# A macaron block on one core: fp16 halves for the second low-rank matrix, the first base block's split moved, the bias added in two halves

## The chip, the cores and the metric

The kernel runs on one core of one Trainium2 chip. A core has a matrix engine (PE, with its weight loads shown as PEld), a vector engine (DVE), a scalar engine (ACT), a general engine (POOL) and a queue engine (SP) that here issues most of the transfers. They run side by side and wait for each other through semaphores. The metric is the device time of one execution in microseconds; the time before is the median of three runs.

## The reference: what is computed

The input x is 2 x 1024 tokens of 1024 features, float32. Three residual steps follow one another, each on a layer norm of x without weights:

```python
x = x + 0.5 * ffn(layernorm(x))
x = x + attention(layernorm(x))
x = x + 0.5 * ffn(layernorm(x))
```

The feed-forward step is a dense product with a bias and a mixture of eight low-rank pairs, of which a gate picks two per token:

```python
gate_logits = einsum('bsd,ed->bse', x, gate_w)            # 8 experts
weights, selected = top_k(gate_logits, 2)                 # softmax over the two
result = einsum('bsd,od->bso', x, base_w) + base_b        # 1024 x 1024
low = einsum('bsd,erd->ebsr', x, lora_A)                  # rank 16 per expert
lora_out = einsum('ebsr,eor,bse->bso', low, lora_B, w_full)
result = result + 2.0 * lora_out
```

Attention is causal, with 32 query heads and 8 key and value heads of 32 features and rotary positions. Both feed-forward steps use the same weights.

## The kernel before

**Tiles and precision.** The 2048 tokens are 16 tiles of 128. Dense products run in fp16 on split operands: a matrix is scaled by a power of two and written as a high half `hi` and a low half `lo = value - hi`, and a product is three matmuls, high by high, high by low, low by high (L361 to L363). `split` (L195) makes the halves of a weight: the high half on ACT (L200) or, for every fourth slice, on POOL (L197), the low half on DVE (L202). `pow2` (L167) finds the scale: squares summed on ACT (L171), the sum over all partitions with a small matmul (L176), a maximum on DVE (L178), a square root on POOL (L179), and then a few one-column operations that give the scale `S` and its inverse `INV` (L187).

**The feed-forward weights.** The base matrix is held in SBUF as two blocks of 512 output columns, `wb[:, n]`; `prep_base(n)` scales and splits block n in eight slices. `prep_gate` does the same for the gate and the first low-rank matrix together (`ag`). `prep_lora` splits the second low-rank matrix, 128 x 1024, into `lbh` and `lbl`. These two are of the type fp32r, a 4-byte type that PE takes, and are scaled with the base blocks' own scales, so that their product can be summed in the same PSUM bank.

**One feed-forward step** is `ffn` (L393), 32 times in all (16 tiles, two steps). First comes the gate product into `psa` (L395, the `misc` tile), then the bias is added to the tile's x on POOL (L396), and the gate's choice is worked out in some fifteen small operations (L399 to L419) that end in `lw`, the weighted low-rank activations. Then for each half n the dense product of 24 matmuls into `pd`, the transposed `lw` split into `lh` and `ll` (L434 to L438, once), three matmuls with `lbh` and `lbl` into the same bank (L441 to L443), and the update of x on DVE (L444), which needs the bias added.

**The layer norm** (`layernorm`, L331) takes statistics on DVE (L334, L336), a reciprocal root on POOL (L340), writes the normed tile on ACT (L352) and splits it: the high half on POOL (L313; for tiles 0 and 1 on ACT, L311), the low half on DVE (L314). A transposing transfer (L317) then brings both halves to the layout that PE needs (`tt`). The first three of these transfers and the loads traced before L776 are kept in SP's queue in program order.

**The order of the work.** The program is written as generators that are stepped by hand: in the prologue the weights are loaded, scaled and split while tiles 0 to 2 run their first step; in the main part, for each tile of attention, pieces of the dense stages are put between the attention units. Within what the program's order and its extra edges leave open, a planner orders the instructions of each engine at build time by priority and by its own estimate of their times. `tc.issue_after(ins)` adds an edge: what is traced inside comes behind `ins` on its engine. The prologue uses such edges: `marks` remembers the last layer norm's instructions, and in `prep_base(0)` the slices from the second on come behind tile 1's `xn` and `hi` on ACT and behind its `nb` and `lo` on DVE. In the program text the order of the prologue is: gate and first base block loaded, tile 1 loaded, layer norm of tile 0, gate prepared, second base block and second low-rank matrix loaded, tile 2 loaded, layer norm of tile 1, bias loaded, `prep_base(0)`, the key and value weights' loads on ACT's queue, `prep_base(1)`, `prep_lora`, the loads of Wo and of Wq's first half, layer norm of tile 2.

Of the kernel before, what the change touches and what calls it, by code (L numbers as in the profile page):

```python
# [9 lines left out]
FP = mybir.dt.float32  # L10
FPR = mybir.dt.float32r
HP = mybir.dt.float16
I32 = mybir.dt.int32
AF = mybir.ActivationFunctionType
# [26 lines left out]
def kernel(  # L41
# [94 lines left out]
    lbh = wres.tile([P, D], FPR)  # L136
    lbl = wres.tile([P, D], FPR)
# [29 lines left out]
    def pow2(aps, junk, name):  # L167

        am = small.tile([P, 2], FP, name="am")
        for j, (ap, jk) in enumerate(zip(aps, junk)):  # L170
            nc.scalar.activation(jk, ap, AF.Square, accum_out=am[:, j : j + 1])  # L171
        sq = small.tile([P, 1], FP, name="sq")
        nc.vector.tensor_tensor(sq, am[:, 0:1], am[:, 1:2], ALU.add)
        nc.vector.tensor_scalar(sq, sq, 2.0**-120, 2.0**120, ALU.max, ALU.min)
        every = p_s2.tile([P, GRP, P], FP, name="s2")[:, 0, :]
        nc.tensor.matmul(every, lhsT=sq.to_broadcast([P, P]), rhs=ident, start=True, stop=True)  # L176
        ar = small.tile([P, 1], FP, name="ar")
        nc.vector.tensor_reduce(ar, every, AX.X, ALU.max)  # L178
        nc.gpsimd.tensor_tensor(ar, ar, half, ALU.pow)  # L179
        e = small.tile([P, 1], FP, name="e")  # L180
        nc.vector.tensor_scalar(e.bitcast(I32), ar.bitcast(I32), 0x7F800000, None, ALU.bitwise_and)
        tag = "_".join(map(str, name))
        s = const.tile([P, 1], FP, name="s_" + tag)
        nc.vector.reciprocal(s, e)
        nc.vector.tensor_scalar(s, s, 16384.0, None, ALU.mult)
        inv = const.tile([P, 1], FP, name="i_" + tag)
        nc.gpsimd.tensor_scalar(inv, e, 1.0 / 16384.0, 0.0, ALU.mult, ALU.add)  # L187
        S[name], INV[name] = s, inv

    marks = {}  # L190

    def mark(name):
        return tc.issue_after(marks[name].ins) if name else nullcontext()

    def split(hi, lo, src, s, k, after=(None, None)):  # L195
        if k % 4 == 3:
            nc.gpsimd.tensor_scalar(hi, src, s, 0.0, ALU.mult, ALU.add)  # L197
        else:
            with mark(after[0]):
                nc.scalar.activation(hi, src, AF.Copy, scale=s)  # L200
        with mark(after[1]):
            nc.vector.scalar_tensor_tensor(lo, src, s, hi, ALU.mult, ALU.subtract)  # L202

    def prep_base(n, sts):
        pow2(sts, [wb[:, n, 0, h * HK : (h + 1) * HK, :] for h in range(2)], ("b", n))
        for k in range(KB):
            after = (None, None)
            if n == 0 and k > 0:
                after = ("xn", "nb") if k == 1 else ("hi", "lo")
            split(wb[:, n, 0, k, :], wb[:, n, 1, k, :], sts[k // HK][:, k % HK, :], S["b", n], k, after)  # L210
        u = const.tile([P, 1], FP, name=f"uf{n}")
        nc.gpsimd.tensor_scalar(u, INV["b", n], 0.5 / XS, 0.0, ALU.mult, ALU.add)
        S["uf", n] = u

    def prep_gate(sts):
# [6 lines left out]
        inva2 = const.tile([P, 1], FP)  # L222
        nc.gpsimd.tensor_scalar(inva2, INV["a",], 2.0, 0.0, ALU.mult, ALU.add)
        S["cg"], S["inva2"] = cg, inva2

    def prep_lora(st):
        for n in range(2):
            c = bass.ts(n, 512)
            nc.scalar.activation(lbh[:, c], st[:, c], AF.Copy, scale=S["b", n])
            nc.vector.scalar_tensor_tensor(  # L230
                lbl[:, c], st[:, c], S["b", n], lbh[:, c].bitcast(FP), ALU.mult, ALU.subtract
            )
        nc.scalar.mul(bb, bb, 0.5)
# [63 lines left out]
    class Split:  # L297
# [7 lines left out]
        def add(self, src, act=False):  # L305
# [4 lines left out]
            if act:  # L310
                marks["hi"] = nc.scalar.copy(hi, src)  # L311
            else:
                nc.gpsimd.tensor_scalar(hi, src, 1.0, 0.0, ALU.mult, ALU.add)  # L313
            marks["lo"] = nc.vector.tensor_tensor(self.hl[:, (2 * i + 1) * w : (2 * i + 2) * w], src, hi, ALU.subtract)  # L314
# [16 lines left out]
    def layernorm(xt, act=False, n=1):  # L331
# [15 lines left out]
        marks["nb"] = nc.vector.scalar_tensor_tensor(nb, mv[:, 0:1], -1.0, rs, ALU.mult, ALU.mult)  # L347
        xn = fpool.tile([P, D], FP, name="xn")
        sp = Split(n)
        for i in range(n):  # L350
            c = bass.ts(i, D // n)
            marks["xn"] = nc.scalar.activation(xn[:, c], xt[:, c], AF.Identity, bias=nb, scale=rs)  # L352
# [40 lines left out]
    def ffn(xt, tt, done):  # L393
        psa = p_misc.tile([P, 512], FP, name="misc")
        yield from dense(psa[:, 0 : P + E], tt, lambda k: (ag[:, 0, k, :], ag[:, 1, k, :]))  # L395
        nc.gpsimd.tensor_tensor(xt, xt, bb, ALU.add)  # L396
# [29 lines left out]
        for n in range(2):  # L426
# [5 lines left out]
            if n == 0:  # L432
                pst = p_misc.tile([P, 512], FP, name="misc")
                nc.tensor.transpose(pst[:, 0:P], lw.rearrange("p e r -> p (e r)"), ident)  # L434
                lh = small.tile([P, P], FPR, name="lh", bufs=LB)
                ll = small.tile([P, P], FPR, name="ll", bufs=LB)
                nc.scalar.copy(lh, pst[:, 0:P])
                nc.vector.tensor_tensor(ll, pst[:, 0:P], lh.bitcast(FP), ALU.subtract)  # L438
# [312 lines left out]
    gst = [agst[:, h] for h in range(2)]  # L751
    b0 = [piece(h - 2, [wb_in[:, 0:512]], h, nc.sync) for h in range(2)]
# [3 lines left out]
    prep_gate(gst)  # L756
    b1 = [piece(3 + h, [wb_in[:, 512:1024]], h, nc.sync) for h in range(2)]
    lst = xp.tile([P, D], FP, name="xt")
    pin(nc.sync.dma_start(out=lst, in_=lb_in))
# [3 lines left out]
    prep_base(0, b0)  # L763
# [239 lines left out]
```

## Time and profile before

| what | value |
|---|---|
| median of 3 runs (lowest, highest) | 1538.43 us (1531.92, 1540.04) |
| the profiled execution's own time | 1540.01 us |
| its span | 1538.2 us |
| mean granted PE clock | 0.984 |
| PE, DVE, ACT, POOL busy | 1434.5, 1080.9, 691.1, 480.0 us |
| first dense product of the base block starts | 25.80 us |
| first attention score matmul starts | 152.74 us |
| PE idle before the third dense product (DVE L444 ends it) | 43.61 to 53.05 us |

The page gives each engine's busy time and, in slices of 1/40 of the span, its busy share in tenths. The chain of work that ended last follows the program back from its last instruction to what released each step. A group row has the line, engine and operation, output and inputs by the program's names, shapes and types, the count, the busy time and mean duration, and after the bar the idle time of the engine just before, with what ended it. A row of waits has who waited for whom, the total in us, the times and the longest. A timeline row has the start and the duration in us, and in brackets the idle time before. Matmuls overlap in their pipeline, so the distance between starts tells their cost, not the duration.

### The profile page before, as it was taken

How to read it: one execution, taken by the hardware profiler on the slowest of the kernel's cores; microseconds unless marked ns; L12 is line 12 of the kernel's file. 1: busy time of each engine (PE TensorE's matmuls, PEld its weight loads, DVE VectorE, ACT ScalarE, POOL GpSimd, SP SyncE). 2: the span in 40 equal slices, each digit the busy share in tenths (PEclk: the TensorE clock that was granted, in tenths of full speed). 3: DMA queues.
4: the chain of work that ended last, by engine and by line, in shares of the span. 5: the costliest groups of instructions: out<-in, count | busy, mean ns of one | idle time of the engine just before them, and what ended most of it. 6: DMA issues, size and time to landing. Idle time of an engine off the chain costs nothing.

```text
span 1538.2 us, 39420 instructions
## 1 busy us (share of the span) xinstructions
PE 1434.5 (93%) x16594; PEld 846.2 (55%) x16594; DVE 1080.9 (70%) x2382; ACT 691.1 (45%) x1276; POOL 480.0 (31%) x678
## 2 busy tenths in 40 slices
PE   3687889899999999999999998999999999999997
PEld 2333445455656566666654454555656656666543
DVE  5968666958768577777664866867768577776553
ACT  7453334444444454454550334444445445555420
POOL 2544332524324133232131433433333232221221
PEclk9998999999999999999999999999999999999999
DMA  9776797969383763855647769566493753553551
GB/s 301 250 207 185 172 242 190 235 166 242 84 254 96 209 173 79 238 106 146 184 116 244 178 189 257 157 196 203 111 256 75 220 145 97 194 132 96 112 180 42
DMA packets 297186, 267.57 MB, mean 174 GB/s; under 512 B 262576, under 2 KB 265648, under 8 KB 276528
## 3 DMA queue, kind: packets, MB, share of 16 engines
q1 hardware_dynamic: 293456, 252.47, 61.5%
q10 hardware_dynamic: 3552, 12.58, 2.1%
q8 instruction: 130, 2.13, 0.6%
q14 instruction: 48, 0.39, 0.1%
HBM read 181.63 MB, written 20.45 MB: 131 GB/s over the span
## 4 chain that ended last, share of the span: by engine, by line
PE 70%; DVE 11%; DMA 10%; issue 3%; POOL 2%; ACT 2%; SPq 1%; ACTq 0%; DVEq 0%; POOLq 0%
PE av L630 14%; PE pd L361 12%; PE pd L362 12%; PE pd L363 12%; PE s L568 8%; PE s L683 7%; DMA qt<-qst 5%; DMA ws<-wstr 2%; DVE mx L585 2%; DVE hl L314 2%; DMA tt<-hl 2%; DVE rc L639 1%; PE pd L441 1%; PE pd L442 1%; PE pd L443 1%
## 5 line engine op out<-in xcount | busy, mean ns | idle before, releaser
L689 ACT ACTIVATE p<-s,cs 128x512 f32<-128x512 f32 x576 | 380.0, 688 | 279.4 <-PE s L683 276.2
L585 DVE TENSOR_REDUCE mx<-s 128x4 f32<-128x512 f32 x480 | 316.4, 676 | 182.0 <-PE s L568 155.9
L630 PE MATMUL av<-p,va 128*32 128x128 f32 x4608 | 236.6, 277 | 2.3 <-POOL p L691 1.3
L361 PE MATMUL pd<-ws,tt 128*128 128x512 f16 x592 | 225.4, 381 | 13.8 <-DMA ws<-wstr 9.4
L630 PE MATMUL av<-p,ones 128*32 128x128 f32 x4608 | 232.1, 273 | 0.0
L362 PE MATMUL pd<-ws,tt 128*128 128x512 f16 x592 | 225.2, 380 | 0.0
L363 PE MATMUL pd<-ws,tt 128*128 128x512 f16 x592 | 224.6, 380 | 0.0
L361 PEld LDWEIGHTS <-tt 128*128 128x128 f16 x1360 | 134.2, 99 | 163.3 <-DMA tt<-hl 28.1
L568 PE MATMUL s<-kts,qt 96*128 96x128 f16 x2304 | 200.0, 220 | 15.3 <-DMA qt<-qst 10.3
L361 PE MATMUL pd<-wb,tt 128*128 128x512 f16 x512 | 196.1, 383 | 17.2 <-DVE xt L444 11.7
L362 PEld LDWEIGHTS <-tt 128*128 128x128 f16 x1360 | 134.2, 99 | 140.4 <-issue 25.0
L683 PE MATMUL s<-qt,kts 128*128 128x512 f16 x576 | 201.9, 382 | 9.3 <-DMA qt<-qst 7.8
L568 PEld LDWEIGHTS <-qt 96*128 96x128 f16 x2304 | 149.9, 98 | 101.8 <-issue 37.7
L363 PEld LDWEIGHTS <-tt 128*128 128x128 f16 x1360 | 134.1, 99 | 129.3 <-issue 7.0
L362 PE MATMUL pd<-wb,tt 128*128 128x512 f16 x512 | 195.9, 383 | 2.2 <-DVE wb L202 2.2
L363 PE MATMUL pd<-wb,tt 128*128 128x512 f16 x512 | 195.7, 382 | 0.0
L630 PEld LDWEIGHTS av<-p,va 128*32 128x32 f32 x4608 | 122.4, 109 | 66.0 <-issue 54.8
L646 POOL TENSOR_TENSOR tt<-o,tt 128x128 f16<-128x128 f32 x128 | 62.7, 490 | 305.1 <-ACT tt L645 305.1
L691 POOL TENSOR_SCALAR_AFFINE_SELECT p<-p 128x512 f32<-128x512 f32 x128 | 85.9, 672 | 198.2 <-ACT p L689 197.1
L639 DVE RECIPROCAL rc<-o 128x128 f32<-128x128 f32 x128 | 121.0, 945 | 37.2 <-ACT o L637 36.9
L630 PEld LDWEIGHTS av<-p,ones 128*32 128x32 f32 x4608 | 138.2, 110 | 0.1
L580 POOL TENSOR_SCALAR_AFFINE_SELECT sm<-sm 128x512 f32<-128x512 f32 x96 | 67.8, 706 | 216.1 <-ACT sm L579 213.5
(164 smaller groups left out, 1815.6 us busy)
## 6 DMA issues: line engine op xcount, KB each, us to landing
ws<-wstr SPq DMA_DIRECT2D x148, 1024.0 KB, 5.9
wstr<-ws ACTq DMA_DIRECT2D x9, 1024.0 KB, 6.5
xt<-in_x_dram SPq DMA_DIRECT2D x16, 512.0 KB, 3.7
out_dram<-xt SPq DMA_DIRECT2D x15, 512.0 KB, 3.1
qt<-qst SPq DMA_TRANSPOSE x256, 3.0
ws<-in_wb_dram SPq DMA_DIRECT2D x2, 1024.0 KB, 8.4
qst<-in_wb_dram SPq DMA_DIRECT2D x2, 1024.0 KB, 7.9
st<-in_wo_dram SPq DMA_DIRECT2D x2, 1024.0 KB, 11.3
```

The lines of the kernel that those rows point to most:

```text
L361: nc.tensor.matmul(ps, lhsT=th, rhs=wh, start=(k == 0), stop=False)
L362: nc.tensor.matmul(ps, lhsT=th, rhs=wl, start=False, stop=False)
L363: nc.tensor.matmul(ps, lhsT=tl, rhs=wh, start=False, stop=(last and k == KB - 1))
L568: nc.tensor.matmul(ps[:, h, :], lhsT=q[0 : 3 * DH, h, :], rhs=KT[b0 + j][0 : 3 * DH, g, :], start=(not pem or h == 0), stop=not pem,)
L580: nc.gpsimd.affine_select(out=sm, in_=sm, compare_op=ALU.is_ge, fill=-3.0e38, base=0, pattern=[[0, GRP], [-1, P]], channel_multiplier=1,)
L585: nc.vector.tensor_reduce(mx[:, j, :], ps, AX.X, ALU.max)
L630: prev = nc.tensor.matmul(av[rows, i, :], lhsT=w, rhs=p32[:, h, :], start=(us[0][0] == 0 and n == 0 and i == 0), stop=(us[-1][0] == L - 1 ...
L639: nc.vector.reciprocal(rc, o[:, 1, :])
L646: nc.gpsimd.tensor_tensor(c.low(g), o2, c.high(g), ALU.subtract)
L683: ins = nc.tensor.matmul(ps.rearrange("p h k -> p (h k)"), lhsT=KT[b0 + j][:, g, :], rhs=q.rearrange("p h k -> p (h k)"), start=True, stop ...
L689: nc.scalar.activation(p32, ps, AF.Exp, scale=cs)
L691: nc.gpsimd.affine_select(out=p32, in_=p32, compare_op=ALU.is_ge, fill=0.0, base=0, pattern=[[0, GRP], [1, P]], channel_multiplier=-1,)
```

## The change

Three things are altered.

- **The second low-rank matrix in fp16.** `lbh`, `lbl`, `lh` and `ll` become fp16. The matrix gets a scale of its own (`pow2` on the loaded tile, name `l`), and so `pow2` has a new argument `least`, a floor under the base block's own measure: for block 0 it is worked out from `INV["a"]` and `INV["l"]`, for block 1 from `INV["b", 0]`. `inva2`, the factor in the gate's last step, now holds the low-rank scale and block 0's scale too, and `prep_lora` uses two column scales, `S["l"]` for the first half and `INV["b", 0] * S["l"] * S["b", 1]` for the second.
- **The prologue's order.** The second low-rank matrix is loaded ahead of the first base block instead of behind the second; its `pow2` comes behind `prep_gate`; `prep_base(0)` is written ahead of tile 2's load and of tile 1's layer norm; `marks` and the edges made with it are gone.
- **The bias** is added to the tile in two instructions of 512 columns instead of one of 1024.

```diff
--- before.py
+++ after.py
@@ -1,5 +1,5 @@
 from collections import deque
-from contextlib import ExitStack, nullcontext
+from contextlib import ExitStack
 
 import concourse.bass as bass
 import concourse.tile as tile
@@ -8,7 +8,6 @@
 from concourse._compat import with_exitstack
 
 FP = mybir.dt.float32
-FPR = mybir.dt.float32r
 HP = mybir.dt.float16
 I32 = mybir.dt.int32
 AF = mybir.ActivationFunctionType
@@ -133,8 +132,8 @@
 
     wb = wres.tile([P, 2, 2, KB, 512], HP)
     ag = wres.tile([P, 2, KB, P + E], HP)
-    lbh = wres.tile([P, D], FPR)
-    lbl = wres.tile([P, D], FPR)
+    lbh = wres.tile([P, D], HP)
+    lbl = wres.tile([P, D], HP)
     wstr = dram.tile([5, 2, P, 2, KB // 2, 512], HP)
     HK = KB // 2
     S, INV = {}, {}
@@ -164,7 +163,7 @@
             c += n
         return st
 
-    def pow2(aps, junk, name):
+    def pow2(aps, junk, name, least=None):
 
         am = small.tile([P, 2], FP, name="am")
         for j, (ap, jk) in enumerate(zip(aps, junk)):
@@ -179,6 +178,8 @@
         nc.gpsimd.tensor_tensor(ar, ar, half, ALU.pow)
         e = small.tile([P, 1], FP, name="e")
         nc.vector.tensor_scalar(e.bitcast(I32), ar.bitcast(I32), 0x7F800000, None, ALU.bitwise_and)
+        if least is not None:
+            nc.vector.tensor_tensor(e, e, least, ALU.max)
         tag = "_".join(map(str, name))
         s = const.tile([P, 1], FP, name="s_" + tag)
         nc.vector.reciprocal(s, e)
@@ -187,27 +188,28 @@
         nc.gpsimd.tensor_scalar(inv, e, 1.0 / 16384.0, 0.0, ALU.mult, ALU.add)
         S[name], INV[name] = s, inv
 
-    marks = {}
-
-    def mark(name):
-        return tc.issue_after(marks[name].ins) if name else nullcontext()
-
-    def split(hi, lo, src, s, k, after=(None, None)):
+    def split(hi, lo, src, s, k):
         if k % 4 == 3:
             nc.gpsimd.tensor_scalar(hi, src, s, 0.0, ALU.mult, ALU.add)
         else:
-            with mark(after[0]):
-                nc.scalar.activation(hi, src, AF.Copy, scale=s)
-        with mark(after[1]):
-            nc.vector.scalar_tensor_tensor(lo, src, s, hi, ALU.mult, ALU.subtract)
+            nc.scalar.activation(hi, src, AF.Copy, scale=s)
+        nc.vector.scalar_tensor_tensor(lo, src, s, hi, ALU.mult, ALU.subtract)
 
     def prep_base(n, sts):
-        pow2(sts, [wb[:, n, 0, h * HK : (h + 1) * HK, :] for h in range(2)], ("b", n))
+
+        least = const.tile([P, 1], FP, name=f"lb{n}")
+        if n == 0:
+            nc.vector.scalar_tensor_tensor(least, INV["a",], 2.0**32, INV["l",], ALU.mult, ALU.mult)
+        else:
+            nc.vector.tensor_scalar(least, INV["b", 0], 16384.0, None, ALU.mult)
+        pow2(sts, [wb[:, n, 0, h * HK : (h + 1) * HK, :] for h in range(2)], ("b", n), least)
+        if n == 0:
+            inva2 = const.tile([P, 1], FP)
+            nc.vector.scalar_tensor_tensor(inva2, INV["a",], 2.0, INV["l",], ALU.mult, ALU.mult)
+            nc.vector.tensor_tensor(inva2, inva2, S["b", 0], ALU.mult)
+            S["inva2"] = inva2
         for k in range(KB):
-            after = (None, None)
-            if n == 0 and k > 0:
-                after = ("xn", "nb") if k == 1 else ("hi", "lo")
-            split(wb[:, n, 0, k, :], wb[:, n, 1, k, :], sts[k // HK][:, k % HK, :], S["b", n], k, after)
+            split(wb[:, n, 0, k, :], wb[:, n, 1, k, :], sts[k // HK][:, k % HK, :], S["b", n], k)
         u = const.tile([P, 1], FP, name=f"uf{n}")
         nc.gpsimd.tensor_scalar(u, INV["b", n], 0.5 / XS, 0.0, ALU.mult, ALU.add)
         S["uf", n] = u
@@ -219,17 +221,16 @@
             split(ag[:, 0, k], ag[:, 1, k], sts[h], S["a",], 0)
         cg = const.tile([P, 1], FP)
         nc.gpsimd.tensor_scalar(cg, INV["a",], 1.0 / XS, 0.0, ALU.mult, ALU.add)
-        inva2 = const.tile([P, 1], FP)
-        nc.gpsimd.tensor_scalar(inva2, INV["a",], 2.0, 0.0, ALU.mult, ALU.add)
-        S["cg"], S["inva2"] = cg, inva2
+        S["cg"] = cg
 
     def prep_lora(st):
+        c = const.tile([P, 2], FP, name="sl")
+        nc.vector.tensor_copy(c[:, 0:1], S["l",])
+        nc.vector.scalar_tensor_tensor(c[:, 1:2], INV["b", 0], S["l",], S["b", 1], ALU.mult, ALU.mult)
         for n in range(2):
-            c = bass.ts(n, 512)
-            nc.scalar.activation(lbh[:, c], st[:, c], AF.Copy, scale=S["b", n])
-            nc.vector.scalar_tensor_tensor(
-                lbl[:, c], st[:, c], S["b", n], lbh[:, c].bitcast(FP), ALU.mult, ALU.subtract
-            )
+            h, s = bass.ts(n, 512), c[:, n : n + 1]
+            nc.scalar.activation(lbh[:, h], st[:, h], AF.Copy, scale=s)
+            nc.vector.scalar_tensor_tensor(lbl[:, h], st[:, h], s, lbh[:, h], ALU.mult, ALU.subtract)
         nc.scalar.mul(bb, bb, 0.5)
 
     KV = [wk_in, wv_in]
@@ -308,10 +309,10 @@
             src = src[:, i * w : (i + 1) * w]
             hi = self.hl[:, 2 * i * w : (2 * i + 1) * w]
             if act:
-                marks["hi"] = nc.scalar.copy(hi, src)
+                nc.scalar.copy(hi, src)
             else:
                 nc.gpsimd.tensor_scalar(hi, src, 1.0, 0.0, ALU.mult, ALU.add)
-            marks["lo"] = nc.vector.tensor_tensor(self.hl[:, (2 * i + 1) * w : (2 * i + 2) * w], src, hi, ALU.subtract)
+            nc.vector.tensor_tensor(self.hl[:, (2 * i + 1) * w : (2 * i + 2) * w], src, hi, ALU.subtract)
             m = 2 * KB // self.n
             pin(
                 nc.sync.dma_start_transpose(
@@ -344,12 +345,12 @@
         rs = small.tile([P, 1], FP, name="rs")
         nc.vector.tensor_tensor(rs, n1, r, ALU.mult)
         nb = small.tile([P, 1], FP, name="nb")
-        marks["nb"] = nc.vector.scalar_tensor_tensor(nb, mv[:, 0:1], -1.0, rs, ALU.mult, ALU.mult)
+        nc.vector.scalar_tensor_tensor(nb, mv[:, 0:1], -1.0, rs, ALU.mult, ALU.mult)
         xn = fpool.tile([P, D], FP, name="xn")
         sp = Split(n)
         for i in range(n):
             c = bass.ts(i, D // n)
-            marks["xn"] = nc.scalar.activation(xn[:, c], xt[:, c], AF.Identity, bias=nb, scale=rs)
+            nc.scalar.activation(xn[:, c], xt[:, c], AF.Identity, bias=nb, scale=rs)
             sp.add(xn, act)
         return sp
 
@@ -393,7 +394,9 @@
     def ffn(xt, tt, done):
         psa = p_misc.tile([P, 512], FP, name="misc")
         yield from dense(psa[:, 0 : P + E], tt, lambda k: (ag[:, 0, k, :], ag[:, 1, k, :]))
-        nc.gpsimd.tensor_tensor(xt, xt, bb, ALU.add)
+        for n in range(2):
+            c = bass.ts(n, 512)
+            nc.gpsimd.tensor_tensor(xt[:, c], xt[:, c], bb[:, c], ALU.add)
 
         lg = small.tile([P, E], FP, name="lg")
         nc.scalar.activation(lg, psa[:, P : P + E], AF.Copy, scale=S["cg"])
@@ -432,10 +435,10 @@
             if n == 0:
                 pst = p_misc.tile([P, 512], FP, name="misc")
                 nc.tensor.transpose(pst[:, 0:P], lw.rearrange("p e r -> p (e r)"), ident)
-                lh = small.tile([P, P], FPR, name="lh", bufs=LB)
-                ll = small.tile([P, P], FPR, name="ll", bufs=LB)
+                lh = small.tile([P, P], HP, name="lh", bufs=LB)
+                ll = small.tile([P, P], HP, name="ll", bufs=LB)
                 nc.scalar.copy(lh, pst[:, 0:P])
-                nc.vector.tensor_tensor(ll, pst[:, 0:P], lh.bitcast(FP), ALU.subtract)
+                nc.vector.tensor_tensor(ll, pst[:, 0:P], lh, ALU.subtract)
                 yield
             c = bass.ts(n, 512)
             nc.tensor.matmul(ps, lhsT=lh, rhs=lbh[:, c], start=False, stop=False)
@@ -749,18 +752,19 @@
                 )
             )
     gst = [agst[:, h] for h in range(2)]
+    lst = xp.tile([P, D], FP, name="xt")
+    pin(nc.sync.dma_start(out=lst, in_=lb_in))
     b0 = [piece(h - 2, [wb_in[:, 0:512]], h, nc.sync) for h in range(2)]
     load_x(1)
     a1 = [stage_a1(t) for t in range(3)]
     next(a1[0])
     prep_gate(gst)
+    pow2([lst[:, bass.ts(h, 512)] for h in range(2)], [lbh[:, bass.ts(h, 512)] for h in range(2)], ("l",))
     b1 = [piece(3 + h, [wb_in[:, 512:1024]], h, nc.sync) for h in range(2)]
-    lst = xp.tile([P, D], FP, name="xt")
-    pin(nc.sync.dma_start(out=lst, in_=lb_in))
+    prep_base(0, b0)
     load_x(2)
     next(a1[1])
     pin(nc.sync.dma_start(out=bb, in_=bias_in.partition_broadcast(P)))
-    prep_base(0, b0)
     stage(2, 0, 0, nc.scalar)
     stage(2, 1, 1, nc.scalar)
     prep_base(1, b1)
```

## The prediction

> **What bounds the kernel now.** I read four views: the page's shares and its slices, the engine totals cut at 160 and 300 us, the waits of PE in those stretches, and the groups and timelines of the touched lines. The page first:
>
> ```profile
> PE 1434.5 (93%) x16594; PEld 846.2 (55%) x16594; DVE 1080.9 (70%) x2382; ACT 691.1 (45%) x1276; POOL 480.0 (31%) x678
> PE   3687889899999999999999998999999999999997
> DVE  5968666958768577777664866867768577776553
> ```
>
> Each digit is 38.5 us. PE is short of work only in the first four slices. The totals cut by stage say the same: PE is busy 106.4 of the first 160 us, 124.2 of the next 140, and 1203.9 of the last 1238.2. So the kernel is a prologue that waits (53.6 us of idle PE) and a long stretch in which PE leaves only 34.3 us. A nanosecond of PE work taken out after 160 us is worth about 0.96 of itself (1328.1 busy of 1378.2); a wait taken from another engine is worth at most what PE idles for it. What PE waits for, first to 160 us, then from 300 us (total, times, longest):
>
> ```profile
> PE misc L361 <- DMA tt<-hl: 16.8, 2, 9.4
> PE pd L361 <- DVE xt L444: 11.7, 3, 9.4
> PE pd L361 <- ACT wb L200: 4.9, 1, 4.9
> ...
> PE misc L361 <- DMA tt<-hl: 4.4, 3, 2.1
> PE s L568 <- DVE mx L585: 2.8, 6, 0.8
> ```
>
> **Part 1: fp16 for the second low-rank matrix.** 3 matmuls of 128x512 in 64 blocks change type. The last two blocks stand side by side at the end of the PE timeline (start, duration):
>
> ```profile
> 1531.82 0.38 PE L362 MATMUL pd<-wb,tt 128*128 128x512 f16 x1
> 1532.04 0.38 PE L363 MATMUL pd<-wb,tt 128*128 128x512 f16 x1
> 1532.07 0.58 PE L441 MATMUL pd<-lbh,lh 128*128 128x512 f32 x1
> 1532.49 0.39 PE L442 MATMUL pd<-lbl,lh 128*128 128x512 f32 x1
> 1532.72 0.39 PE L441 MATMUL pd<-lbh,lh 128*128 128x512 f32 x1
> 1532.95 0.39 PE L442 MATMUL pd<-lbl,lh 128*128 128x512 f32 x1
> 1533.18 0.63 PE L443 MATMUL pd<-lbh,ll 128*128 128x512 f32 x2
> ```
>
> Read the starts, not the durations: the 0.58 only begins early. fp16 matmuls start 0.216 us apart, these 0.23. Six at 0.216 behind 1532.04 would end at 1532.04 + 6 x 0.216 + 0.38 = 1533.72; they end at 1533.81, so 0.045 us per triple. Where another matmul follows (159.68 to 160.83 us: L363, three of these, two of fp16) the spacing is 1.147 against 5 x 0.216 = 1.080: 0.067. The weight load of these takes 190 ns in the median (L441), that of fp16 98 to 99 ns. Here a rule is to be weighed. The Trainium skill (TensorE: Matmul & The Clock Gate, LDWEIGHTS) prices a load by its columns alone, 128/1.2 = 107 ns whatever the type, which would hide all of it and make this part worth 0; its section on weight-path modes excepts fp32 from the fast load. The row has 190 against 99, so I go by the rows: 64 x (0.045 to 0.067) = 2.9 to 4.3 us of PE, middle 3.5, times 0.96: **-3.3 us** (ends 0 and -4.3). L229, L230, L437 and L438 write fp16 in place of a 4-byte type: L200 and L202 do this at the same size (0.71 and 0.75 us against 0.71 and 0.72), so nothing.
>
> **Part 2: the bias add in halves.** In most blocks L396 follows L313 on POOL, and holds up the low half L314 on DVE, which feeds the transpose that PE waits for:
>
> ```profile
> 1343.84 1.04 POOL L313 TENSOR_SCALAR hl<-xn 128x1024 f16<-128x1024 f32 x1 [1.45 <-ACT xn L352]
> 1344.85 2.36 POOL L396 TENSOR_TENSOR xt<-xt,bb 128x1024 f32<-128x1024 f32 x1
> ...
> 1344.92 3.38 DVE L314 TENSOR_TENSOR hl<-xn,hl 128x1024 f16<-128x1024 f32 x1 [0.65 <-POOL hl L313]
> ```
>
> L314 takes 1.21 us when free. 20 of its 48 take over 2.5 us, 40.5 us above 1.21 in all. Size of a half: L646 does 128 elements in 0.42 us at the least, L396 1024 in 2.35, so 2.15 ns an element and 512 in 1.25; two are 0.15 dearer, 32 x 0.15 = 4.8 us on a POOL busy 31%. Does DVE get in between the halves? The Trainium skill (GPSIMD Engine Reference, Instruction dispatch) says that a following Pool instruction starts on each of its cores as soon as the share of the one before is done, no barrier between. Taken alone that lets the second half follow at once, and L314 ends 0.15 later than now: 32 x 0.15 = up to 4.8 us lost on DVE. The trace shows the case, three adds back to back:
>
> ```profile
> 41.30 8.29 POOL L396 TENSOR_TENSOR xt<-xt,bb 128x1024 f32<-128x1024 f32 x3
> ...
> 40.70 3.94 DVE L202 SCALAR_TENSOR_TENSOR wb<-qst,s_b,wb 128x512 f16<-128x512 f32 x2 [0.59 <-POOL wb L197]
> 44.77 6.04 DVE L202 SCALAR_TENSOR_TENSOR wb<-qst,s_b,wb 128x512 f16<-128x512 f32 x3
> ```
>
> An add here is 2.76 us apart instead of 2.35, and one L202 passes at each boundary (ends at 44.64, 47.40 and 50.14). So DVE does get in, and the later add waits. L314 then ends about 1.1 us earlier, 20 x 1.1 = 22 us of DVE. PE idles for few of them: behind the held L314 at 850.6 (idle 1.34 us), 1344.9 (0.84), 1511.4 (2.10, with the 4.2 us transpose between), around 282 to 292 (0.72 and 1.99), and behind L644 at 925.5 (2.05). At most 1.1 from each, and half of it for the last two: 1.1 + 0.84 + 1.1 + 1.1 + 0.6 = 4.7. Where a second such operation follows (L510 then L314 at 114; L595 then L314 at 872) the second half catches it and nothing is won. I take **-4 us**. Ends: +1 (POOL's 4.8 us on the path at the place of its 2% in the chain, or the rule) and -10 (L314 is 2% of the chain, 31 us, a third of that).
>
> **Part 3: the prologue.** *Added*: a scale for the second low-rank matrix. Two squares on ACT (like L171's 0.65 + 0.19 each): 1.7 us. DVE: some 14 small operations at 0.15 to 0.29 (sum, clamp, reduce, mask, two for the scale, the floor, the maximum twice, two for inva2, two for the pair of scales): 2.3 us. POOL a power (0.55) less one product (0.19); PE two small matmuls (0.77 at 9.34). Cover: ACT is idle 2.3 us before 19.18 and 1.6 before 22.03, DVE idle most of the time to 22 us, PE from 10.1 to 17.5; without it 2 to 3 us. On the path stay the maximum (0.15) and the data: 512 KB go ahead of the base block in SP's queue, 0.5 us of issue and at the 300 to 350 GB/s of those microseconds 1.5 to 1.7 of transfer. ACT is behind the data anyway (second square of block 0 at 14.90, landed 13.6), so the scale comes at about 23.0 instead of 22.34.
>
> *Moved*: eight splits of block 0 (six L200 of 0.71, two L197, eight L202 of 0.75) go ahead of tile 1's norm in program order and lose their order edges. ACT starts its six at 25.03 now, after one square and L311 of tile 1; it could start at 23.0. For: -2 us to the first dense product, which L200 and L202 hold (PE idle 4.87 and 2.16). Against: tile 1's L311 falls behind 3.8 us of ACT and its L314 behind 5.5 us of DVE, so its transpose leaves SP up to 5.5 us after 26.41. Behind it in SP's queue stand the bias and two Wo loads (31.6 to 33.6); the Wq loads wait till 50.2 for their buffer anyhow. The transpose lands at 35.1, and PE starts tile 1's product at 35.68, so PE is late by those 5.5. What hides this is the next hole: PE idles from 43.61 to 53.05, for L444, which stands on DVE behind all eight L202 of block 1. Gone, that cover costs 5.5. The adds at 41.3 shift with the bias, and L444 has 8 us of room after the first. **+1 us**, ends -3 and +7.
>
> **Sum.** -3.3 - 4 + 1 = -6.3 us. The profiled execution took 1540.0 (span 1538.2, 1.8 around it), 1.6 above the median: 1533.7 for it, 1538.4 - 6.3 = **1532 us** in the median. The planner makes the order anew from its own estimates, and a new order of the prologue is the part that no row prices.
>
> **Rivals.**
> - *The DVE release spreads* (faster): all of the 10 us of chain in L314 comes back, block 0 starts 2 us earlier, PE saves 3.8: -15.8, 1523 us. For: DVE is 11% of the chain, mostly attention maxima behind such rows. Against: PE idles only 34.3 us after 300.
> - *Tile 1 late* (slower): its norm falls behind the splits of block 0, and its product and gate come 5.5 us later; tile 1 then also enters the waiting row of three transposes at 111 to 139 us later, so the hole that hides it moves along instead of shrinking. Two such slips, 5.5 at 35 us and as much again at the 9.4 us hole before 122, less gains of 3, are +8 to +12: 1548 us. It decides once the slip passes what the 9.44 us hole covers. For: 16.8 us of PE waits for these transposes before 160. Against: the hole is bound by DVE, not by tile 1.
> - *Nothing arrives*: the loads are hidden as the rule has it, the second half catches what follows: 1538 us.
>
> **How the numbers follow.** The sum as worked out 0.36, the spread 0.26, tile 1 late 0.28, nothing 0.10. 0.5% is 7.7 us, about what a measurement here can tell from no change: bounds 1530.7 and 1546.1. Faster: 0.24 of the spread and 0.12 of the sum, 0.36. Slower: 0.24 of tile 1 late. Same 0.40. Range 1520 to 1550: the spread's centre less 3, the late case's centre plus 2; about 2 in 10 lie outside. The likeliest case by itself: 1526 to 1538.
>
> **What would show it.** Lora matmuls 0.216 apart with 99 ns loads; two L396 halves of 1.25 us with L314 ending near 2.2 us after its start; first dense product at 23.5 to 25.5 us; tile 1's transpose issued at 27 to 32; the hole before 53 us still ended by L444. Wrong if L314 stays at 3.4, or if first attention scores (152.7 now) come later than 157 or earlier than 148.

## The result and the profile after

The changed kernel takes 1525.88 us in the median of six runs (1522.40 to 1528.67), the kernel before 1538.62 in its six (1531.92 to 1540.09). The ratio is **0.9909**, 95% interval 0.9892 to 0.9926: about 14 us faster. The sum of the prediction was -6.3 and its time 1532. The profiled execution of after took 1522.65 us, span 1520.9, granted clock 0.985 against 0.984; it lies 17.4 below that of before, more than the ratio says, and parts read from single profiles below carry some us of scatter.

The shares of the page of after:

```profile
PE 1428.8 (94%) x16596; PEld 832.9 (55%) x16596; DVE 1067.4 (70%) x2396; ACT 691.1 (45%) x1280; POOL 496.6 (33%) x711
```

PE is busy 5.7 us less, and its idle time fell from 103.7 to 92.1. DVE does 14 instructions more and is busy 13.5 less; POOL is busy 16.6 more. Time that DVE stood under the adds thus went over to POOL. By the same stages as in the prediction, PE idles 49.4 us to 160 us (53.6 before), 14.8 from there to 300 (15.8), and 27.9 after that (34.3).

What PE waits for, first to 160 us, then from 300 us (total, times, longest):

```profile
PE s L175 <- DVE sq L173: 24.0, 5, 8.1
...
PE pd L362 <- DMA tt<-hl: 3.7, 1, 3.7
PE pd L362 <- DVE xt L447: 3.4, 1, 3.4
PE misc L362 <- DMA tt<-hl: 1.5, 1, 1.5
...
PE s L571 <- DVE mx L588: 2.1, 4, 0.8
...
PE misc L362 <- DMA tt<-hl: 1.5, 2, 1.1
```

The gate product's wait for a transpose (`misc`) went from 16.8 to 1.5 before 160 us and from 4.4 to 1.5 after 300; the 11.7 us behind the residual update are 3.4. But 24.0 us of waits for the sums of squares of weights (L173, in `pow2`) have come up in their place, so that PE idles in all only 4.2 less before 160 us; what is won there is that it is further on by then.

The end of the PE timeline of after (start, duration) and its loads for the low-rank matmuls (count, min/median/max ns):

```profile
1514.89 0.38 PE L364 MATMUL pd<-wb,tt 128*128 128x512 f16 x1
1515.11 0.38 PE L444 MATMUL pd<-lbh,lh 128*128 128x512 f16 x1
1515.33 0.38 PE L445 MATMUL pd<-lbl,lh 128*128 128x512 f16 x1
...
1515.97 0.59 PE L446 MATMUL pd<-lbh,ll 128*128 128x512 f16 x2
```

```profile
L444 PEld LDWEIGHTS <-lh x64: 95/98/99, 43.8 to 1515.3; 128*128 128x128 f16 x64
```

The spacing is the 0.216 us of the base product and the load is 98 ns, as forecast. A feed-forward step's layer norm near the end, POOL and DVE of after:

```profile
1495.53 1.04 POOL L314 TENSOR_SCALAR hl<-xn 128x1024 f16<-128x1024 f32 x1 [2.25 <-ACT xn L353]
1496.54 3.47 POOL L399 TENSOR_TENSOR xt<-xt,bb 128x512 f32<-128x512 f32 x2
1496.97 1.92 DVE L315 TENSOR_TENSOR hl<-xn,hl 128x1024 f16<-128x1024 f32 x1
```

The low half (L315) took 1.92 us here where the place shown of before took 3.38, and the two halves of the add took 3.47 together where the whole took 2.36: the second one waited for DVE. The same line over the whole run, before and after (min/median/max ns):

```profile
L314 DVE TENSOR_TENSOR hl<-xn,hl x48: 1159/1643/3387, 11.8 to 1511.4; 128x1024 f16<-128x1024 f32 x48
```

```profile
L315 DVE TENSOR_TENSOR hl<-xn,hl x48: 1160/1667/2299, 14.3 to 1497.0; 128x1024 f16<-128x1024 f32 x48
```

The median hasn't moved, but none is over 2.3 us, where 20 were over 2.5. Before, the 48 held 43.9 us above 1.21; after, 24.4.

### The profile page after: what moved, and what is told of

Its sections match the earlier page's. It is cut to its first block, busy times and chain, and to the rows that moved or that the text cites. A ratio compares the mean times of both kernels' runs of the same rounds, so it can differ in the third digit from the quotient of the medians.

```text
span 1520.9 us, 39480 instructions
## 1 busy us (share of the span) xinstructions
PE 1428.8 (94%) x16596; PEld 832.9 (55%) x16596; DVE 1067.4 (70%) x2396; ACT 691.1 (45%) x1280; POOL 496.6 (33%) x711
## 4 chain that ended last, share of the span: by engine, by line
PE 74%; DVE 10%; DMA 8%; issue 2%; POOL 2%; ACT 1%; SPq 1%; DVEq 0%; POOLq 0%; ACTq 0%
PE av L633 15%; PE pd L362 13%; PE pd L363 13%; PE pd L364 13%; PE s L571 8%; PE s L686 7%; DMA ws<-wstr 3%; DMA qt<-qst 3%; DVE ws L196 1%; DVE mx L588 1%; DVE hl L315 1%; DMA tt<-hl 1%; PE pd L444 1%; PE pd L446 1%; PE pd L445 1%
## 5 line engine op out<-in xcount | busy, mean ns | idle before, releaser
L649 POOL TENSOR_TENSOR tt<-o,tt 128x128 f16<-128x128 f32 x128 | 55.5, 434 | 295.6 <-ACT tt L648 295.5
L583 POOL TENSOR_SCALAR_AFFINE_SELECT sm<-sm 128x512 f32<-128x512 f32 x96 | 62.1, 647 | 204.2 <-ACT sm L582 203.9
```

Of the source, the lines that this page charges most:

```text
L583: nc.gpsimd.affine_select(out=sm, in_=sm, compare_op=ALU.is_ge, fill=-3.0e38, base=0, pattern=[[0, GRP], [-1, P]], channel_multiplier=1,)
L649: nc.gpsimd.tensor_tensor(c.low(g), o2, c.high(g), ALU.subtract)
```

## Experiments

Two theories stood against each other. **Release**: an add on POOL holds up the DVE instruction beside it, chiefly the low half, until the current POOL instruction ends; halves shorten the hold, and the time follows. **Order**: every edit makes the planner lay out the whole program anew, and a new order is worth some us by chance or by the moved prologue, whatever the halves do. Of the change's three edits, **h** is the add in halves, **t** the fp16 types, **o** all the rest: the low-rank matrix's own scale and earlier load, the moved split, no marks. All eight combinations were measured.

### The halves alone

```diff
-        nc.gpsimd.tensor_tensor(xt, xt, bb, ALU.add)
+        for c in (bass.ts(0, 512), bass.ts(1, 512)):
+            nc.gpsimd.tensor_tensor(xt[:, c], xt[:, c], bb[:, c], ALU.add)
```

> The kernel before with the bias add in two halves and nothing else. Theory 1 (prologue): the change won about 6 us before the main part, by the new order, and the halves only free PE where it idles behind a held low half: 4 us less than before, 1534.5. Theory 2 (release): the halves let DVE run earlier everywhere, prologue included, and are most of the change: 8 to 10 us less, 1529. L314 ends about 2.25 us after its start in both.

Measured: 1531.52 us against 1540.99, ratio 0.9932 (0.9915 to 0.9948). This one line brings about three quarters of the whole change. Its low halves:

```profile
L314 DVE TENSOR_TENSOR hl<-xn,hl x48: 1159/1646/2299, 11.2 to 1508.5; 128x1024 f16<-128x1024 f32 x48
```

### The types alone

```diff
-    lbh = wres.tile([P, D], FPR)
-    lbl = wres.tile([P, D], FPR)
+    lbh = wres.tile([P, D], HP)
+    lbl = wres.tile([P, D], HP)
...
-                lh = small.tile([P, P], FPR, name="lh", bufs=LB)
-                ll = small.tile([P, P], FPR, name="ll", bufs=LB)
+                lh = small.tile([P, P], HP, name="lh", bufs=LB)
+                ll = small.tile([P, P], HP, name="ll", bufs=LB)
```

> The kernel before with lbh, lbl, lh and ll in fp16 and nothing else (scales and order as before). Both theories: PE saves 2.9 to 4.3 us in the 192 matmuls, 3.3 us of it at the end, 1535. If the loads are hidden anyway: 1538.5.

Measured: 1539.95 against 1540.99, 0.9990 (0.9980 to 1.0000): 1 to 1.5 us, if anything, where 3.3 was forecast.

### The prologue alone

The changed kernel with the types of before and the whole add:

```diff
-        for n in range(2):
-            c = bass.ts(n, 512)
-            nc.gpsimd.tensor_tensor(xt[:, c], xt[:, c], bb[:, c], ALU.add)
+        nc.gpsimd.tensor_tensor(xt, xt, bb, ALU.add)
...
-    lbh = wres.tile([P, D], HP)
+    lbh = wres.tile([P, D], FPR)
```

> The changed kernel with the bias add whole and the 4-byte type put back, so that only the prologue's order, its loads and the scale of its own are changed against before. Theory 1: the first base block's splits end by 28 us and the second's by 44, PE's hole before 53 us shrinks, and 5 to 7 us less than before, 1532. Theory 2: tile 1's late transpose eats what the splits gain, within 2 us of before.

Measured: 1541.39 against 1540.99, 1.0005 (0.9992 to 1.0017). The first attention score starts at 145.9 us instead of 152.7, so the prologue is nearly 7 us ahead, and the end knows nothing of it. By tile 0's last score the lead is gone: it starts at 200.2, in before at 193.8. Between these two scores PE idles 11.4 us, in before 5.0. The waits of PE from 160 to 215 us, of o and then of before, and of SP's queue in o from 145 to 205:

```profile
PE pd L362 <- DMA ws<-wstr: 5.1, 2, 3.0
```

```profile
PE pd L361 <- DMA ws<-wstr: 1.2, 1, 1.2
```

```profile
SPq L374 <- DMA wstr<-ws: 11.3, 1, 11.3
```

PE waits there for weights (`ws`) read back from DRAM, and their load waits in SP's queue for the split weights to be written there. PE came earlier, the weights did not. The clock takes its part too: between the two scores its mean is 0.94 in o and 1.00 in before. That is two stretches of 3.4 us at half clock, which cost up to 3.4 us of work.

### The marks alone

The kernel before without its edges in `prep_base(0)`, as a control for the order:

```diff
-            if n == 0 and k > 0:
-                after = ("xn", "nb") if k == 1 else ("hi", "lo")
```

> The kernel before without its order edges (marks) on the first base block; the program's order, types and bias add as before. Theory 1 (the order of the first block decides): the split starts as soon as the scale is there, some 2 us earlier, and a part of the order's gain is seen, 2 to 4 us less than before. Theory 2 (edges don't matter, the planner had put tile 1's norm ahead in any case): within 2 us.

Measured: 1541.28, 1.0001 (0.9989 to 1.0012). A new order, the same time, and the same granted clock (0.984 in the mean).

### Two of three

The halves with the types: the edits of the first two experiments together, in before.

```diff
-    lbh = wres.tile([P, D], FPR)
+    lbh = wres.tile([P, D], HP)
...
-        nc.gpsimd.tensor_tensor(xt, xt, bb, ALU.add)
+        for c in (bass.ts(0, 512), bass.ts(1, 512)):
+            nc.gpsimd.tensor_tensor(xt[:, c], xt[:, c], bb[:, c], ALU.add)
```

> The kernel before with the halves and with fp16, the prologue's order, its scales and its loads as before. If the parts add up (halves alone 0.9932 of before, types alone 0.999): 0.992, 1529 against 1541. If the types pay in full only once PE no longer waits for the low halves: 0.990, that is the whole of the change.

Measured: 1529.44 against 1540.55, 0.9923 (0.9907 to 0.9938).

The halves with the prologue: the changed kernel with the four tiles of the low-rank product (`lbh`, `lbl`, `lh`, `ll`) of the 4-byte type.

```diff
-    lbh = wres.tile([P, D], HP)
+    lbh = wres.tile([P, D], FPR)
```

> The changed kernel with the 4-byte type put back: halves and the prologue's order. If the parts add up (halves 0.9932, order alone 1.0005): 0.9937, 1531. If the order pays only together with the halves, because without them the whole adds hold the splits of the second block: 0.991 or less.

Measured: 1529.02, 0.9919 (0.9906 to 0.9932).

The types with the prologue: the changed kernel with the whole add.

```diff
-        for n in range(2):
-            c = bass.ts(n, 512)
-            nc.gpsimd.tensor_tensor(xt[:, c], xt[:, c], bb[:, c], ALU.add)
+        nc.gpsimd.tensor_tensor(xt, xt, bb, ALU.add)
```

> The changed kernel with the bias add whole: fp16 and the prologue's order. If the parts add up: 0.9995, 1540. If order and types win something of their own that the halves don't need: 0.997 or less.

Measured: 1541.19, 1.0005 (0.9990 to 1.0021): **without the halves the change is worth nothing**.

The table cuts each profile into three. *Tail* goes from the start of the last score matmul (L683 in before) to the end of the last matmul; *body* from tile 2's last score matmul to the one where the tail begins; *head* is the rest of the span. The last column is the granted PE clock, as a share of the full clock, over all executions of a kernel; before has 0.9840 (19) on the chip of the kernels with two of three.

| kernel | ratio to before | head us | body us | tail us | granted clock, mean (runs) |
|---|---|---|---|---|---|
| before | 1 | 317.2 | 1169.5 | 51.5 | 0.9835 (51) |
| without marks | 1.0001 | 317.0 | 1168.1 | 51.6 | 0.9837 (13) |
| t | 0.9990 | 321.2 | 1168.6 | 51.3 | 0.9834 (21) |
| o | 1.0005 | 319.4 | 1172.1 | 51.4 | 0.9807 (21) |
| t and o | 1.0005 | 317.5 | 1168.5 | 49.7 | 0.9791 (14) |
| h | 0.9932 | 318.7 | 1166.2 | 47.6 | 0.9840 (6) |
| h and t | 0.9923 | 314.9 | 1163.0 | 47.4 | 0.9830 (6) |
| h and o | 0.9919 | 312.1 | 1165.0 | 47.4 | 0.9832 (5) |
| after (h, t and o) | 0.9909 | 311.9 | 1161.5 | 47.5 | 0.9845 (6) |

The five kernels with the whole add lie within 0.15% of each other, 2.3 us, each in an order of its own; the four with halves lie together 0.7 to 0.9% lower. So a new order by itself does not bring the change's time. It isn't without effect, though: o and t and o run at a lower granted clock than before on the same chip, by 0.0028 and 0.0049 (standard errors 0.0006 and 0.0009). Times 1541 us, this is up to 4.3 and 7.6 us that these orders win elsewhere and pay back in clock; the estimate is an upper one, since half clock costs nothing while PE idles. The kernels with halves run within 0.001 of the clock of before, so their gain is no gain of clock. Halves are worth 0.68% alone, 0.67% beside t, 0.86% beside o, 0.96% beside both (differences of the ratios; 0.1% is 1.5 us); the larger values beside o go with the clock that o loses without them. In the mean of four against that of five they gain 4.1 us in the head, 5.4 in the body and 3.6 in the tail. In the same means PE idles 5.6, 3.1 and 2.1 us less in these three, and loses up to 1.4, 1.0 and 1.4 us less to half clock; what PE does in head and body differs from kernel to kernel, so these parts don't add up to the gains. The tail is the firm one: its values agree to 0.3 us but for one kernel.

### Quarters

```diff
-        for n in range(2):
-            c = bass.ts(n, 512)
+        for n in range(4):
+            c = bass.ts(n, 256)
             nc.gpsimd.tensor_tensor(xt[:, c], xt[:, c], bb[:, c], ALU.add)
```

> The changed kernel with the bias add in four instructions of 256 columns. If the hold on the low half is what the halves took away, a quarter of 0.70 us lets L315 start 0.55 us earlier once more, so it ends near 1.7 us in place of 2.25, and half of the gain comes again: 2 to 4 us less than the changed kernel, at 0.988 of before. If the new order that the planner makes is what paid, the quarters land anywhere within 5 us of the changed kernel.

Measured: 1523.82 against 1540.55, 0.9883 (0.9863 to 0.9902), where after has 0.9909. The low half is nearly free, with 11.1 us above 1.21 left of 24.4:

```profile
L315 DVE TENSOR_TENSOR hl<-xn,hl x48: 1156/1241/1758, 14.1 to 1500.5; 128x1024 f16<-128x1024 f32 x48
```

### The whole add behind the low half

This takes the hold on the low half away with no halving: the add of before waits until the tile's low half is done.

```diff
-            marks["lo"] = nc.vector.tensor_tensor(...)
+            self.lo = marks["lo"] = nc.vector.tensor_tensor(...)
...
-        nc.gpsimd.tensor_tensor(xt, xt, bb, ALU.add)
+        add = nc.gpsimd.tensor_tensor(xt, xt, bb, ALU.add)
+        tc.add_manual_dep(add.ins, tt.lo.ins.name, ..., reason="low")
```

> The kernel before, its bias add whole, but made to wait for the low half of the tile's layer norm (L314). If the hold on the low half is what costs: no L314 is over 1.3 us any more, and at least the gain of the halves is there, 0.9932 of before or less, near 0.990. If the halves paid by the other order that the planner made of 32 more instructions, or by shorter holds on other DVE operations: the add now holds those for its full 2.35 us, and the time is within 3 us of before.

Measured: 1532.32 against 1541.15, 0.9941 (0.9920 to 0.9963), about the halves' gain with one instruction per add. Its low halves, and one add that waits:

```profile
L314 DVE TENSOR_TENSOR hl<-xn,hl x48: 1161/1225/1648, 11.2 to 1510.5; 128x1024 f16<-128x1024 f32 x48
```

```profile
1510.54 1.22 DVE L314 TENSOR_TENSOR hl<-xn,hl 128x1024 f16<-128x1024 f32 x1
...
1511.84 2.35 POOL L396 TENSOR_TENSOR xt<-xt,bb 128x1024 f32<-128x1024 f32 x1 [1.74 <-DVE hl L314]
```

So taking the hold off the low half is worth about 9 us in the order that this kernel got. Its low halves are not wholly free, as was expected: 12 of 48 take over 1.3 us (28 in before). But of the 43.9 us above 1.21 only 4.2 are left, where the halves leave 24.4 and win no less. Time does not follow the low half alone, then; the halves also shorten the holds on other DVE operations, and how much of their gain lies there is not shown. This kernel's granted clock is a little higher than that of before (0.9855 in the mean against 0.9834), by the same estimate up to 3.2 us of its gain. Its tail is 46.4 us, a little shorter than with halves.

### No bias add

The kernel before without the add. The bias is missing from the output, so this is not a faster kernel but the price of the add.

```diff
-        nc.gpsimd.tensor_tensor(xt, xt, bb, ALU.add)
```

> The kernel before without the bias add (L396 left out, so the bias is missing from the output; all else as before). It bounds what the add costs. If the low halves are all of it: as with the add behind the low half, 0.990 to 0.989. If DVE's other held operations count as much: 0.986 or less (of 69 us that DVE loses under the adds, 40 are the low halves').

Measured: 1521.07 against 1541.15, 0.9875 (0.9855 to 0.9895). The 32 adds cost about 19 us end to end, though POOL is busy 31% of the span. This lies between the two values expected, so the low halves are not all of it. Halves give back a good half of that, and the tail without any add (46.4 us) is that of the add behind the low half.

### The changed kernel with the add behind, whole and in quarters

```diff
-        for n in range(2):
-            c = bass.ts(n, 512)
-            nc.gpsimd.tensor_tensor(xt[:, c], xt[:, c], bb[:, c], ALU.add)
+        add = nc.gpsimd.tensor_tensor(xt, xt, bb, ALU.add)
+        tc.add_manual_dep(add.ins, tt.lo.ins.name, ..., reason="low")
```

> The changed kernel with the add whole again and made to wait for the low half (L315). If the hold on the low half decides: as fast as the changed kernel with its halves or 1 to 3 us faster, 0.989 to 0.991 of before. If it decides only because the halves shorten every hold: 3 us or more slower than the changed kernel, 0.993 or more.

Measured: 1521.90 against 1541.15, 0.9882 (0.9861 to 0.9903). With the quarters it is the best version found. Each ratio was taken against before on its own chip, their intervals touch that of after, and the three were not timed side by side, so that either beats the change is likely and not shown.

The same with the add in quarters, each behind the low half:

```diff
-        for n in range(2):
-            c = bass.ts(n, 512)
-            nc.gpsimd.tensor_tensor(xt[:, c], xt[:, c], bb[:, c], ALU.add)
+        for n in range(4):
+            c = bass.ts(n, 256)
+            add = nc.gpsimd.tensor_tensor(xt[:, c], xt[:, c], bb[:, c], ALU.add)
+            tc.add_manual_dep(add.ins, tt.lo.ins.name, ..., reason="low")
```

> The changed kernel with the add in quarters (256 columns), each made to wait for the low half. Both cures together: the low half free at 1.21 us, other operations held for 0.7 us at most. If hold time on DVE is what is left to win: below the quarters alone (0.9883), 0.986. If PE's idle time behind low halves was already gone with the quarters: 0.988 to 0.989.

Measured: 1529.42, 0.9923 (0.9902 to 0.9943). Both theories missed it: two remedies together are worse than either alone. Its tail is short (46.4 us) and its body 1165.8. Nor is it the clock, 0.983 in the mean like that of the quarters. What costs it the 6 us was not found.

## Why the prediction was wrong

The sign was right and the size was not: 14 us instead of 6.3. Going from before to after as h, then o, then t, the ratios give -10.5, -2.0 and -1.5 us; the last two lie within the intervals of their ratios.

**Part 2, the halves, failed in its size.** The step at fault is the listing "1.1 + 0.84 + 1.1 + 1.1 + 0.6 = 4.7" and the -4 taken from it, where h alone measured -10.5. The mechanism was right: the low half went from 3.38 to about 2.2 us at its longest, the second half of the add waits, and the reading of the three adds in the prologue beat the rule of instructions without a barrier. Wrong was to price only the PE idle seen next to a held row: in the means above PE idles 10.8 us less over the run, more than twice the listing, and the half clock that follows idle stretches stood in the sum at nothing.

- *Tail.* The sum counted one item of 1.1 here; it measured 4.0 (51.5 to 47.5). The gap before the last gate product fell from 2.10 to 1.1 us: that is the item of 1.1. Another idle of 1.01 us at 1494, behind a held L314 of 3.12 us, was on no list and is gone. A third item, about 1.7, is in no row of waits: behind the gap of 2.10 the clock was halved, which is shown below. The remaining 0.3 us are within what the profiles differ by.
- *Body.* The listing has 2.5 us; 5.4 came in the mean. No single wait carries it: between 300 and 1480 us the gate's wait for a transpose went from 1.3 us to 0.2 in h alone and the wait for a maximum (L585) from 2.8 to 1.1, but the one for the query strip (`qst`) rose from 7.1 to 9.1. Where in the body it lies is not settled.
- *Head.* The listing credits it with about 1.1 us, for the gaps around 282 to 292. It gained 4.1 in the mean, unevenly. The first attention score of h alone starts at 148.5 us against 152.7: the halves let more of the L202 through beside the prologue's adds, and PE's hole that lasted to 53.05 us ends at 49.5. But in h's profile this lead is gone by tile 2's last score (314.4 us against 312.8); up to there PE idles 5.7 us less, and half clock costs up to 3.4 more. In h and o and in after the head is 5 us shorter than in before.

The end at -10, a third of the 31 us that L314 has in the chain, came near. It does not ask for an idle PE beside each held row, which is to its credit, but its third was not worked out, and that it hit is luck.

**Part 3, the prologue, missed by little in time and by much inside.** +1 was forecast; it is 0 alone (1.0005) and -2 beside the halves, neither clear of noise. Its first step went the wrong way: the scale of block 0 was to come at 23.0 us instead of 22.34 and came at 20.8, and the first dense product starts at 22.7, ahead of the 23.5 to 25.5 given. Tile 1's transpose left at 30.5 us instead of 26.4, inside the 27 to 32 given:

```profile
30.51 3.38 SPq L318 DMA_TRANSPOSE tt<-hl  x1
...
35.97 0.61 PE L362 MATMUL pd<-wb,tt 128*128 128x512 f16 x1 [3.67 <-DMA tt<-hl]
```

The prediction put the whole slip on the landing. But this transfer landed after 5.4 us where that of before took 8.7, so tile 1's product starts at 35.97 instead of 35.68. No later hole had to cover it; what is lost is the 3 us by which the first block was earlier, since PE now waits 3.67 us. The hole to 53.05 has shrunk, as the prologue of after shows on POOL and DVE:

```profile
41.76 8.77 POOL L399 TENSOR_TENSOR xt<-xt,bb 128x512 f32<-128x512 f32 x6 [4.03 <-ACT bb L234]
...
46.87 0.75 DVE L447 SCALAR_TENSOR_TENSOR xt<-pd,uf,xt 128x512 f32<-128x512 f32 x1 [0.56 <-PE pd L446]
```

The update stands at 46.87 us. In place of PE's gap from 43.61 to 53.05 there is one of 1.9 us and, from 54.34, one of 3.4 that the update ends; with o alone the first is 6.4 us. The first attention score came at 137.5, far below the 148 that was named as a sign of error. That the estimate of time was near is luck: the scale, the first product, the landing of the transpose and the hole all came otherwise, and o's lead of 7 us is lost again to the weights from DRAM and to half clock. Beside the halves some of it is kept in the profile (tile 0's last score at 186.8 in h and o, 193.8 in before).

**Part 1, the types, was right in the rows and too high in time.** Spacing and load are as worked out, 0.216 us and 98 ns (the 1.147 us of the prediction's second place stand at 148.53 to 149.67 us in the trace of before, not at 159.68), and the rule that would price the load alike for every type is refuted by 190 against 98. But the four pairs of ratios with and without t differ by 0.10, 0.00, 0.09 and 0.10%: about 1.1 us, where 3.3 was the sum; the pair with 0.00 is the one whose granted clock fell most, from 0.9807 to 0.9791. The step that fell short is "times 0.96", which takes a stretch with 4% idle as one in which PE sets the end. That what PE saves turns into waiting for others is an argument, not shown row by row: the bodies of the four pairs fall by 0.9 to 3.6 us, and one execution each is too few to say where the rest is lost.

**The rivals.** *The DVE release spreads* (1523 us) came nearest, with the mechanism given there: its chance was set to 0.26 because "PE idles only 34.3 us after 300". That argument failed: about a third came before 300 us, a part in the clock, and after 300 us the idle time still fell by 6.4. *Tile 1 late* happened as a slip of 4 us, of which 0.3 reached tile 1's product, since the transfer was the faster one. *Nothing arrives* is out. The measured 1525.88 lies within 1520 to 1550.

**Open.** What costs quarters behind the low half their 6 us; which waits make up the body's gain; how much of the halves' gain comes from other holds than the low half's; and why o and t and o are granted less clock where the adds are whole.

## What to carry to other kernels

Price a POOL instruction on two SBUF tiles by the DVE row it holds up, not by POOL's load: here 32 adds on an engine 31% busy cost about 19 us, and cutting them, or making them wait for the DVE row that feeds the critical transfer, returned about half of it for a line or two. When such a hold goes, look beyond the idle of PE that stands next to it in the trace, above all to what follows: other holds without a visible gap, the prologue, and the clock. And a lead in a prologue counts only if the next transfer can be earlier too: milestones along the run (here the last score of each tile) show where it is given back. Before equal times are read as no effect, compare the granted clocks.

## What the hardware showed

**Half clock follows a stretch of 3.41 us in which PE was busy less than about half.** In all 14 profiles the granted clock changes only on a grid of 3.41 us, which starts at a different point in each run, and it is either 1.00 or 0.50. On this grid, the stretch with the gap before the last gate product and the next one, of before, of t and o, and of after (stretch and length, busy time of PE, PEld, DVE, ACT, POOL, then the granted PE clock, DMA share, GB/s):

```profile
1516.61:1520.02 3.41, 1.35 (x23) 1.35 (x24) 0.75 (x1) 0.00 (x0) 0.00 (x0) 1.00 0.91 245
1520.02:1523.43 3.41, 3.41 (x13) 1.36 (x11) 2.17 (x11) 0.57 (x2) 0.00 (x0) 0.50 0.00 0
```

```profile
1516.42:1519.84 3.41, 1.91 (x27) 1.67 (x28) 0.08 (x1) 0.27 (x1) 0.00 (x0) 1.00 0.69 208
1519.84:1523.25 3.41, 3.41 (x18) 1.52 (x16) 2.17 (x11) 0.30 (x1) 0.00 (x0) 1.00 0.00 0
```

```profile
1501.32:1504.73 3.41, 2.29 (x29) 1.68 (x28) 0.75 (x1) 0.00 (x0) 0.00 (x0) 1.00 0.72 200
1504.73:1508.15 3.41, 3.41 (x19) 1.53 (x17) 2.17 (x11) 0.57 (x2) 0.00 (x0) 1.00 0.08 32
```

In before PE is busy 40% of the first stretch, and the first base matmuls of the last product then run at a granted clock of 0.50 for 3.4 us, 0.43 us apart instead of 0.216, while PE counts as fully busy: that is 1.7 us of work lost which no row of waits shows. In after the gap is 1.1 us, PE is busy 67%, and the clock stays at 1.00. Yet t and o has a gap of 2.2 us at the same place and keeps its clock, and its tail is 1.7 us shorter than that of o (49.7 against 51.4). The grid tells why: it cuts this gap so that PE is still busy 56% of the stretch.

Counted over the 14 profiles from 35 us on, after a stretch at full clock with PE busy below 35% the next was at half clock in all 75 cases; from 35 to 60% in 57 of 125; from 60% up in none of 5706. After a stretch at half clock the next was at full clock in all 138 cases with PE busy 80% or more, and in none of 52 below 70%. The Trainium skill (TensorE: Matmul & The Clock Gate, What's actually happening) has the gate judge windows of about 3.4 us that run freely, and turn to half clock after an idle one. Length and free run agree with the grid here; "idle" has to be read, by these counts, as busy less than about half. So whether a gap of 2 us costs another 1.7 depends on where the grid falls, which changes from run to run.

**DVE passes between two POOL instructions.** With halves the later POOL instruction waits for DVE and not the other way: 64 halves take 111.4 us in after, 1.74 each, where one takes 1.26 at the least, and the 32 whole adds took 78.0. What is held until the current POOL instruction ends is DVE work with two SBUF inputs, like L314 and L202, for which the Trainium skill (GPSIMD Engine Reference, Specifications) names the SBUF interfaces as shared between the two engines; the update from PSUM (L447) is not, with 0.75 us at 46.87 beside the adds and no more than that in any of its 64 times.
